# V2's first half ahead of the second chunk's first row, M's column reads on two queues, and the adding DMA on alternating tile rows

## The chip, the cores and the metric

The kernel runs on one core of a Trainium2 chip. Five engines take part: TensorE (PE in the profile; its weight loads are PEld), VectorE (DVE), ScalarE (ACT), GpSimd (POOL) and SyncE (SP), which issues most of the DMAs. Each engine works through its own instruction list in order; an instruction that waits holds up all that stand behind it on the same engine. DMAs are issued by an engine's queue and then run beside everything else. The metric is the device time of one execution in microseconds; the time given is the median of three runs.

## The reference, cut to what matters

The model is a compressed interaction network over x, a batch of 1024 with 64 features and 16 embedding columns.

```python
h = x0 = x                                     # (1024, 64, 16), float32
for i in range(3):                             # W0: 128 x 64*64, W1, W2: 128 x 64*64
    z = einsum('bfe,bge->bfge', x0, h)         # all products of a feature of x and one of h
    y = einsum('oc,bce->boe', W[i], z.reshape(b, -1, e)) + b[i]
    if i != 2: x_i, h = y[:, :64], y[:, 64:]   # one half is pooled, the other goes on
    else:      x_i = y                         # the last layer is pooled whole
    xs.append(x_i)
out = concat(xs, 1).sum(2) @ fc_w.T + fc_b     # pooled over e, then one number per batch row
```

The first layer's second half h1 is a quadratic form of x. Since the result is a weighted sum over all channels, the last layer can be folded ahead of time: V2 is W2 summed over its 128 output channels with their weights from fc_w, a 64 x 64 matrix, and M is V2 times the second half of W1, so that one more set of 64 quadratic forms of x, called q, stands for the second and third layers. What remains for each batch row is h1 and q (both x⊗x against fixed weights), their product summed over channels and columns, and some small terms.

## The kernel before, in words

**Tiles.** The batch is cut into 32 chunks of 32 rows, so a chunk has 512 columns (32 rows by 16 columns). For a chunk, `xa` holds 128 partitions by 4 by 512: the features, turned by i = 0 to 3. `xb` holds the features turned by 4 times j plus an offset, in four quarters of 128 by 512. A block z = xa * xb[j] (128 x 2048) has four tiles i; a *tile row* j is one block, and four rows hold all products that are needed. Fourteen blocks `z0` to `z13` are handed out in turn from a list (`take`, `used`). The weights `w_all` have 16 tiles (j, i) of 128 x 128: columns 0 to 63 give h1 (W0, made symmetric) and columns 64 to 127 give q (from M). All is float32; the profile shows each matmul as two passes.

**The head** deals with four chunks, in the order c0 to c3 = 2, 3, 0, 1, before M exists. For these only h1 is contracted: `product` (L240) makes a row on VectorE or GpSimd, and `half_contract` (L248; by columns for c0, L257) multiplies it with the first half of the weights. In between lies the making of q's weights:

- V2: eight matmuls in two halves n (L359), each of four matmuls of 32 columns of output partitions, with W2's half n as it was loaded (`w2s[n]`) as their moving operand. VectorE transposes each half's result (L364) into a block and copies the wanted rows into `v2t` (L371, with ScalarE at L372).
- M: eight matmuls of `v2t` with W1 (L387), evicted by ScalarE (L401) and written by DMA into a DRAM tensor `md` (L416 to L425).
- M is read back from `md` in the order of the tiles: `read_rows` (L469) and `read_columns` (L463) fill the two halves of `ms`, each DMA half of the partitions. VectorE adds the two (`q_weights`, L499) into the weights, a tile row at a time, and `head_q_tile` (L281) starts to use them for chunks 0 and 1, whose products are kept for it. `va` (features of M's diagonal) is read from `md` as well.

The code's order is each engine's order here: before the change `half_contract(c1, 0)`, the second chunk's first row, stands ahead of both halves of V2; row 0 and column 0 reads, and the row reads of rows 1 to 3, go out on SyncE and ScalarE, one half each; the six column reads of rows 1 to 3 and the read of `va` go out on SyncE behind `half_contract(c3, ...)`, ahead of the loads of chunk 4. Completion of these DMAs is counted on eight semaphores that are used in turn, so a DMA also waits for the one eight before it.

**The steady state.** From chunk 6 on, 26 chunks go in 13 pairs k = 3 to 15 (chunks a and b). For a pair, both quadratic forms of both chunks come from seven products of combined blocks with combined weights instead of eight: X, B21, B22, T3 are products from VectorE (`w_product`, L644, with sums of quarters at L650), and T2, T1, T4 are sums and differences of such blocks, made by GpSimd (`w_mix`, L661), in place where it can. T4 is used by `p4_run`, the run of matmuls into the PSUM bank `delta` with the first weights' half. Of T4's two tile rows GpSimd adds row 0 itself, and row 1 is added by a DMA that GpSimd issues (L659, `accum_op=add`, 1 MB). The operations of all pairs are put in a list by `at(when, ...)` and emitted in order of `when`; `when` is a position in units of one step, 31 steps to a pair. The table `mixed` holds a pair's seven mixes: T2 row 0, T2 row 1 in two parts, T1 rows 0 and 1, and last T4 row 0 at 18.5 and T4 row 1 at 18.6 (17.5 and 17.6 in the first pair). T4 is T2 with B21 added in place, so GpSimd's last work for a pair is its add of row 0, and then it issues the adding DMA for row 1. The first pair (k = 3) runs `first_window`; of the others those with even k run `a_leads` and those with odd k `o_leads`, which differ in which chunk's matmuls lead. In all, `p4_run`'s last four jobs (`LATE`), which are one tile row, go into the next pair (`first_fill`, `second_fill`).

All matmuls of the steady state go through `mm` (L530). `alpha`, `beta`, `gamma` and `delta` are PSUM banks, of which a pair of matmuls fills the two partition halves in turn.

Of the kernel before, what the change touches and what calls it, by code (L numbers as in the profile page):

```python
# [42 lines left out]
F = 64  # L43
# [7 lines left out]
NI = 4  # L51
NJ = 4
# [12 lines left out]
GROUPS = [(j, i) for j in range(2) for i in range(NI)]  # L65
# [5 lines left out]
def cin_kernel(ctx, tc, xra, xrb, wh, w0r, w1h, w2t, wx1, wx0, vec, lin, out):  # L71
    nc = tc.nc
# [6 lines left out]
    halves = [slice(0, F), slice(F, 128)]  # L79

    def const_tile(name, shape):
        return const.tile(shape, F32, tag=name, name=name)
# [4 lines left out]
    def take(uses=1):  # L87
        n = vacant.pop(0)
        left[n] = uses
        return n  # L90

    def used(n, times=1):
        left[n] -= times
        assert left[n] >= 0
        if left[n] == 0:
            vacant.append(n)
# [21 lines left out]
    for base in (0, 64, -64):  # L118
        nc.gpsimd.affine_select(
            out=shift, in_=shift, compare_op=ALU.not_equal, fill=1.0, base=base,  # L120
# [12 lines left out]
    va, vb, v0 = (const_tile(n, [128, F]) for n in ("va", "vb", "v0"))  # L133
# [8 lines left out]
    def load_xa(c, at=slice(0, NI)):  # L142
        if c not in xas or at.start == 0:
            xas[c] = xp.tile([128, NI, N], F32, tag="xa", name=f"xa_{c}")
        nc.sync.dma_start(  # L145
            out=xas[c][:, at, :],
            in_=bass.AP(
                tensor=xra.tensor, offset=c * XR * N + at.start * N,
                ap=[[N, 128], [1, (at.stop - at.start) * N]],
            ),  # L150
        )

    def quarter(c, j):
        xbs.setdefault(c, {})[j] = xp.tile([128, N], F32, tag="xb", name=f"xb_{c}_{j}", bufs=9)
        return xbs[c][j]

    def load_xb(c, *js):
        for j in js or range(NJ):
            nc.sync.dma_start(out=quarter(c, j), in_=xrb[c, :, j, :])
# [26 lines left out]
    c0, c1, c2, c3 = HEAD  # L186
# [49 lines left out]
    def product(c, j, first=0, last=NI, engine=nc.vector, uses=1):  # L236
        if first == 0:
            zs[c, j] = take(uses)
        at = slice(first, last)
        engine.tensor_tensor(  # L240
            blocks[zs[c, j]][:, at, :], xas[c][:, at, :],
            xbs[c][j].unsqueeze(1).to_broadcast([128, last - first, N]), ALU.mult,
        )

    def half_contract(c, *js, last=None):
        for j in js:
            for i in range(NI):
                nc.tensor.matmul(  # L248
                    accs[c][halves[i % 2]], w_all[:, j * NI + i, 0:64], blocks[zs[c, j]][:, i, :],
                    start=(j == 0 and i < 2), stop=(j == last and i > 1),  # L250
                )
            used(zs[c, j])
# [70 lines left out]
    for i in range(NI):  # L323
# [20 lines left out]
        out=linear, in_=bass.AP(tensor=lin.tensor, offset=lin.offset, ap=[[0, 128], [1, 384]])  # L344
# [2 lines left out]
    product(c1, NJ - 1, engine=nc.gpsimd)  # L347
    for j in (0, 1):
        product(c1, j)
    half_contract(c1, 0)  # L350


    v2b = take()
# [2 lines left out]
    for n in range(2):  # L356
        pv = ps.tile([128, 512], F32, tag=("set", "y")[n], name=f"pv2_{n}")
        for k in range(4):
            nc.tensor.matmul(  # L359
                pv[32 * k : 32 * k + 32], fv2, w2s[n][:, k * 512 : (k + 1) * 512],  # L360
                start=True, stop=True,
                tile_position=(0, 32 * k),
            )
        nc.vector.transpose(v2r[:, n, :], pv)  # L364
        used(w2b[n])


    v2q = v2r.rearrange("p n (s r) -> p (n s) r", r=32)[:, :, 0]
    for h in range(2):
        at = slice(32 * h, 32 * h + 32)  # L370
# [37 lines left out]
    row = EXT * F  # L408

    def m_ap(f1, f2, dims):  # L410
        return bass.AP(tensor=md.tensor, offset=md.offset + f1 * row + f2 * F, ap=dims)
# [3 lines left out]
    for half, queue in enumerate((nc.sync, nc.scalar)):  # L415
        queue.dma_start(  # L416
            out=m_ap(0, 32 * half, [[row, F], [1, 32 * F]]), in_=m_rows[halves[half]]
# [5 lines left out]
        out=m_ap(64, 68, [[row, 4], [4 * F, 7], [1, 4 * F]]),  # L423
        in_=m_rows[0:4, 4 * F :].rearrange("p (k c) -> p k c", c=4 * F),
# [29 lines left out]
    def skewed(f1, f2, dims):  # L454

        at = len(dims) - 2
        return m_ap(f1, f2, dims[:at] + [[row + F, F]] + dims[at:])
# [4 lines left out]
    def read_columns(j, queue, half):  # L462
        queue.dma_start(  # L463
            out=ms[halves[half], 1, j * NI : (j + 1) * NI],
            in_=skewed(0, 16 * half + 4 * (j + 1), [[row, NI], [1, F]]),
        )

    def read_rows(js, queue, half):
        queue.dma_start(  # L469
            out=ms[halves[half], 0].rearrange("p (j i) g -> p j (i g)", i=NI)[:, js],  # L470
            in_=skewed(
                16 * half + 4 * (js.start + 1), 0, [[4 * row, js.stop - js.start], [1, NI * F]]
            ),
        )

    for half, queue in enumerate(queues):
        read_rows(slice(0, 1), queue, half)
        read_columns(0, queue, half)
        read_rows(slice(1, NJ), queue, half)


    new_acc(c3)
# [2 lines left out]
    keep_h1(c2)  # L485
    half_contract(c3, 0, 3, 1, 2, last=2)

    for half in range(2):
        read_columns(1, nc.sync, half)
    for j in (2, 3):  # L490
        for half in range(2):
            read_columns(j, nc.sync, half)
    nc.sync.dma_start(out=va[halves[1]], in_=m_ap(0, 0, [[row + F, F], [1, F]]))
    load_xa(4)
    load_xb(4, 3, 0, 1, 2)

    def q_weights(j):
        at = slice(j * NI, (j + 1) * NI)
        nc.vector.tensor_tensor(w_all[:, at, 64:128], ms[:, 0, at], ms[:, 1, at], ALU.add)  # L499
# [20 lines left out]
    def at(when, fn, *args, **flags):  # L520
        ops.append((when, len(ops), fn, args, flags))
# [103 lines left out]
    FIRST_ROW, SECOND_ROW = GROUPS[:NI], GROUPS[NI:]  # L625

    def w_run(p, out, w, name, start=False, at_t=0, order=GROUPS):
        return [
            (w_job, p, out, w, j * NI + i + at_t, name, start and n == 0)
            for n, (j, i) in enumerate(order)  # L630
        ]
# [7 lines left out]
    wh_all, wq_all = w_all[:, :, 0:64], w_all[:, :, 64:128]  # L639
# [13 lines left out]
    def w_mix(p, j, out, in0, in1, first=0, last=NI):  # L653
        p.setdefault(out, {})
        if j not in p[out]:
            p[out][j] = p["X"][j] if j and p["k"] > 3 else take(9)
        o, x, y = p[out][j], p[in0][j], p[in1][j]
        if in1 == "B21" and j:
            nc.gpsimd.dma_start(out=blocks[o], in_=blocks[y], accum_op=ALU.add)  # L659
            return  # L660
        nc.gpsimd.tensor_tensor(  # L661
            *(blocks[b][:, first:last] for b in (o, x, y)),
            ALU.subtract if in1 == "T3" else ALU.add,
        )
        if last < NI:
            return
        for b in (x, y):
            if b != o:
                used(b)
# [26 lines left out]
    def make_pair(t, p, when, mixed):  # L696
        a, b = p["a"], p["b"]
        for when, c, j, name, uses in (
            (when[0], b, 2, "B22", 5), (when[1], b, 0, None, 0), (when[2], b, 0, "T3", 9),
            (when[3], a, 0, "X", 5), (when[4], b, 3, "B22", 5), (when[5], b, 1, None, 0),  # L700
            (when[6], b, 1, "T3", 9), (when[7], a, 1, "X", 13 if p["k"] > 3 else 5), (when[8], a, 2, "B21", 5),
            (when[9], a, 3, "B21", 5),
        ):
            if name is None:
                at(t + when, w_both, p, j)
                continue
            if name == "B21" and j == 2 and p["k"] == 3:
                at(t + when, w_product, p, c, j, name, uses, engine=nc.gpsimd)
                continue
            if name != "T3":  # L710
                ahead = 3.3 if p["k"] > 4 and name == "B22" and j == 2 else 2.7
                if p["k"] == 3 and name == "X" and j == 1:
                    ahead = 9.1
                at(t + when - ahead, second, c, j)
            at(t + when, w_product, p, c, j, name, uses)
        t2, t1, t4 = ("T2", "X", "T3"), ("T3", "B22", "T2"), ("T2", "T2", "B21")
        for when, j, names in zip(
            mixed, (0, 1, 1, 0, 1, 1, 0), (t2, (*t2, 0, 2), (*t2, 2), t1, t1, t4, t4)
        ):
            at(t + when, w_mix, p, j, *names)  # L720
        at(t + 29, lambda: used(p["B21"][1]))

    def p4_run(p):
        return w_run(p, delta, wh_all, "T2", at_t=2 * NI)

    def first_fill(p):
        return [(lambda: q_extra(p["a"], va, p["beta"]),)] + p4_run(p)[-LATE : -LATE // 2]

    def second_fill(p):
        return p4_run(p)[-LATE // 2 :]  # L730
# [149 lines left out]
    for n, p in enumerate(pairs):  # L880
        t = T0 + SPAN * n
# [54 lines left out]
    t, q = T0 + SPAN * NPAIR, pairs[-1]  # L936
# [184 lines left out]
```

## Time and profile before

| | us |
|---|---|
| median of three runs | 448.66 (447.75, 448.66, 449.8) |
| the profiled execution, its own time | 448.52 |
| its span | 446.7 |
| PE busy | 441.9 (99%) |
| DVE busy | 393.5 (88%) |
| POOL busy | 366.7 (82%) |
| ACT busy | 117.2 (26%) |
| POOL idle ahead of its mixes, released by PE | 28.8 (12 times) |
| xa load, 1024 KB, from issue to landing (median) | 8.9 |
| xb load, 256 KB | 8.5 |
| adding DMA, 1024 KB, 13 of them | 8.1 |
| DMA, mean | 224 GB/s |

The span is the time from the first to the last recorded instruction. In a timeline line the first number is the start in us from the span's start, the second the length, then the engine, the line, the operation, its output and inputs by name, its tile, its forms, and how many such instructions follow one another; in brackets stands the idle time of the engine just ahead and what ended it (`<-DVE z L240`: VectorE's write of a block at line 240). A matmul's end is modelled, its start is recorded, so the distance between starts tells the rate. The granted clock of TensorE is 0.9 and more in all slices of the page.

### The profile page before, as it was taken

The numbers are of one execution on the slowest core, as the hardware profiler recorded it, in microseconds if no ns is written. First come the engines' busy times: TensorE is split into PE (matmuls) and PEld (weight loads), VectorE is DVE, ScalarE is ACT, GpSimd is POOL, SyncE is SP. The second block draws the span as 40 slices with busy tenths as digits, with TensorE's granted clock in tenths as the row PEclk, the third lists the DMA queues.
The fourth block names the chain that finished last, engine by engine and source line by source line (L and its number), as shares of the span: only waits on it lengthen the run. The fifth ranks groups of instructions, "written<-read, shape, count | busy, mean of one in ns | idle before, by whom it ended". The sixth has DMA issues, their size and how long they took to land.

```text
span 446.7 us, 5944 instructions
## 1 busy us (share of the span) xinstructions
PE 441.9 (99%) x2234; PEld 151.8 (34%) x2234; DVE 393.5 (88%) x293; ACT 117.2 (26%) x215; POOL 366.7 (82%) x128
## 2 busy tenths in 40 slices
PE   9999999999999999999999999999999999999997
PEld 5333333333333333333333333333333333333345
DVE  4897699989989989999899979999899998999644
ACT  3163241332223123131312212231231313123211
POOL 5424788998997979799797979979797997979910
PEclk9999999999999999999999999999999999999999
DMA  8996998397949597694949769494976949692400
GB/s 299 416 343 151 331 412 342 93 346 133 357 117 295 167 221 273 137 360 102 303 158 234 268 128 357 105 312 149 232 264 133 372 92 286 223 240 86 98 1 0
DMA packets 35060, 99.85 MB, mean 224 GB/s; under 512 B 6389, under 2 KB 7189, under 8 KB 28441
## 3 DMA queue, kind: packets, MB, share of 16 engines
q1 hardware_dynamic: 32376, 84.90, 53.7%
q0 software_dynamic: 1872, 13.63, 17.4%
q10 hardware_dynamic: 784, 0.95, 0.8%
q8 instruction: 17, 0.28, 0.2%
q14 instruction: 11, 0.08, 0.0%
HBM read 84.20 MB, written 1.64 MB: 192 GB/s over the span
## 4 chain that ended last, share of the span: by engine, by line
PE 91%; DMA 6%; DVE 1%; SPq 0%; issue 0%; DVEq 0%
PE alpha L530 45%; PE delta L530 20%; PE beta L530 11%; PE acc L530 7%; PE q L530 3%; DMA xa<-in_xra 3%; PE acc L281 3%; DMA xb<-in_xrb 2%; PE acc L248 2%; DMA z<-in_w0r 1%; DVE z L240 1%; PE y L530 0%; SPq L145 0%; SPq L195 0%; PE hx L530 0%
## 5 line engine op out<-in xcount | busy, mean ns | idle before, releaser
L661 POOL TENSOR_TENSOR z<-z,z 128x2048 f32<-128x2048 f32 (+1 forms) x78 | 299.9, 3878 | 28.8 <-PE alpha L530 28.8
L530 PE MATMUL alpha<-z,ws 128*64 128x512 f32 x624 | 235.4, 593 | 0.0
L644 DVE TENSOR_TENSOR z<-xa,xp 128x2048 f32<-128x2048 f32 x103 | 231.5, 2279 | 1.2
L530 PEld LDWEIGHTS alpha<-z,ws 128*64 128x64 f32 x624 | 72.4, 137 | 91.0 <-issue 90.5
L530 PE MATMUL delta<-z,w_all 128*64 128x512 f32 x208 | 96.5, 592 | 0.0
L530 PE MATMUL alpha<-z,w_all 128*64 128x512 f32 x208 | 93.4, 593 | 0.0
L530 PE MATMUL beta<-z,w_all 128*64 128x512 f32 x208 | 92.7, 594 | 0.0
L530 PE MATMUL delta<-z,ws 128*64 128x512 f32 x208 | 91.4, 592 | 0.0
L558 ACT COPY xp<-xb 128x512 f32<-128x512 f32 x88 | 51.4, 587 | 127.4 <-DVE z L644 109.2
L240 DVE TENSOR_TENSOR z<-xa,xp 128x2048 f32<-128x2048 f32 (+1 forms) x29 | 45.5, 1619 | 4.3 <-ACT xp L558 3.2
L240 POOL TENSOR_TENSOR z<-xa,xb 128x2048 f32<-128x2048 f32 x6 | 28.2, 4760 | 17.5 <-DMA xb<-in_xrb 17.5
L530 PEld LDWEIGHTS delta<-z,w_all 128*64 128x64 f32 x208 | 28.4, 137 | 32.2 <-issue 32.2
L530 PEld LDWEIGHTS alpha<-z,w_all 128*64 128x64 f32 x208 | 28.1, 137 | 32.0 <-issue 29.5
L530 PEld LDWEIGHTS delta<-z,ws 128*64 128x64 f32 x208 | 28.5, 137 | 27.4 <-issue 25.7
L530 PEld LDWEIGHTS beta<-z,w_all 128*64 128x64 f32 x208 | 28.0, 137 | 27.4 <-issue 27.4
L530 PE MATMUL acc<-z,w_all 128*64 128x512 f32 x128 | 28.1, 592 | 0.0
L248 PE MATMUL acc<-z,w_all 128*64 128x512 f32 x96 | 21.6, 597 | 1.1 <-DVE z L240 1.1
L675 ACT ACTIVATE snap<-alpha,vs 64x512 f32<-64x512 f32 x13 | 8.9, 684 | 50.2 <-PE alpha L530 50.2
L682 DVE SCALAR_TENSOR_TENSOR snap<-alpha,vs,snap 64x512 f32<-64x512 f32 x13 | 9.7, 747 | 12.5 <-PE alpha L530 12.5
L672 ACT COPY snap<-alpha 64x512 f32<-64x512 f32 x13 | 7.6, 581 | 49.2 <-PE delta L530 34.9
L305 DVE TENSOR_REDUCE acc<-uu 128x64 f32<-128x1024 f32 (+2 forms) x19 | 19.6, 1036 | 0.2
L650 DVE TENSOR_TENSOR xp<-xp,xb 128x512 f32<-128x512 f32 x26 | 18.2, 699 | 0.8
(121 smaller groups left out, 357.6 us busy)
## 6 DMA issues: line engine op xcount, KB each, us to landing
xa<-in_xra SPq DMA_DIRECT2D x32, 1024.0 KB, 8.9
xb<-in_xrb SPq DMA_DIRECT2D x128, 256.0 KB, 8.5
z<-z POOLq DMA_DIRECT2D x13, 1024.0 KB, 8.1
e<-in_xra SPq DMA_DIRECT2D x28, 128.0 KB, 8.2
xx<-in_xra SPq DMA_DIRECT2D x28, 128.0 KB, 2.5
z<-in_w2t SPq DMA_DIRECT2D x2, 1024.0 KB, 8.4
z<-in_wx SPq DMA_DIRECT2D x2, 1024.0 KB, 9.9
xa<-in_xra SPq DMA_DIRECT2D x5, 256.0 KB, 4.3
```

The source lines that it names most:

```text
L240: engine.tensor_tensor(blocks[zs[c, j]][:, at, :], xas[c][:, at, :], xbs[c][j].unsqueeze(1).to_broadcast([128, last - first, N]), ALU.mult,)
L248: nc.tensor.matmul(accs[c][halves[i % 2]], w_all[:, j * NI + i, 0:64], blocks[zs[c, j]][:, i, :], start=(j == 0 and i < 2), stop=(j == las ...
L281: nc.tensor.matmul(accs[c][halves[1 - c % 2]], w_all[:, t, 64:128], blocks[zs[c, j]][:, i, :], start=(t == 0), stop=False, skip_group_chec ...
L305: nc.vector.tensor_reduce(acc[rows, of, k, half], uu[rows, of if at is None else at, E * half.start : E * half.stop].rearrange("p k (b e) ...
L530: nc.tensor.matmul(out, w, rhs, start=start, stop=stop, skip_group_check=True)
L558: nc.scalar.copy(bank, xbs[c][j])
L644: engine.tensor_tensor(blocks[b], xas[c], xbs[c][j].unsqueeze(1).to_broadcast([128, NI, N]), ALU.mult)
L650: nc.vector.tensor_tensor(bank, bank, xbs[p["b"]][j], ALU.add)
L661: nc.gpsimd.tensor_tensor(*(blocks[b][:, first:last] for b in (o, x, y)), ALU.subtract if in1 == "T3" else ALU.add,)
L672: nc.scalar.copy(snaps[0][p["O"]], alpha(p))
L675: nc.scalar.activation(snaps[1][p["O"]], alpha(p), AF.Identity, bias=bh1[p["A"]])
L682: nc.vector.scalar_tensor_tensor(hb_, alpha(p), bh1[p["A"]], hb_, ALU.add, ALU.add)
```

## The change: what it does

1. `half_contract(c1, 0)` is taken from ahead of V2 and stands now between V2's two halves: the order on TensorE becomes V2's first half, the second chunk's row 0, V2's second half.
2. The column reads of rows 1 to 3 stand in the loop over the two queues, behind each queue's row reads: SyncE reads half 0, ScalarE half 1. All are ahead of `half_contract(c3, ...)` in the code. The read of `va` goes from ahead of the loads of chunk 4 to behind them.
3. Which row of T4 is added by DMA alternates: row 0 in odd pairs, row 1 in even ones as before (`p["k"] % 2 ^ 1`). Since row 0's place (18.5) is ahead of row 1's (18.6), in odd pairs the DMA is issued ahead of GpSimd's own add. `p4_run` takes the second row first in odd pairs, and the block that the DMA read is given back accordingly.

```diff
     for j in (0, 1):
         product(c1, j)
-    half_contract(c1, 0)
...
         nc.vector.transpose(v2r[:, n, :], pv)
         used(w2b[n])
+        if n == 0:
+            half_contract(c1, 0)
...
         read_rows(slice(0, 1), queue, half)
         read_columns(0, queue, half)
         read_rows(slice(1, NJ), queue, half)
+        for j in range(1, NJ):
+            read_columns(j, queue, half)
...
     half_contract(c3, 0, 3, 1, 2, last=2)
 
-    for half in range(2):
-        read_columns(1, nc.sync, half)
-    for j in (2, 3):
-        for half in range(2):
-            read_columns(j, nc.sync, half)
-    nc.sync.dma_start(out=va[halves[1]], in_=m_ap(0, 0, [[row + F, F], [1, F]]))
     load_xa(4)
     load_xb(4, 3, 0, 1, 2)
+    nc.sync.dma_start(out=va[halves[1]], in_=m_ap(0, 0, [[row + F, F], [1, F]]))
...
         o, x, y = p[out][j], p[in0][j], p[in1][j]
-        if in1 == "B21" and j:
+        if in1 == "B21" and j == p["k"] % 2 ^ 1:
             nc.gpsimd.dma_start(out=blocks[o], in_=blocks[y], accum_op=ALU.add)
             return
...
-        at(t + 29, lambda: used(p["B21"][1]))
+        at(t + 29, lambda: used(p["B21"][p["k"] % 2 ^ 1]))
 
     def p4_run(p):
-        return w_run(p, delta, wh_all, "T2", at_t=2 * NI)
+        order = SECOND_ROW + FIRST_ROW if p["k"] % 2 else GROUPS
+        return w_run(p, delta, wh_all, "T2", at_t=2 * NI, order=order)
```

## The prediction

> **What bounds the kernel now.** I read four views in this order: the page, the chain of work that ended last, the timelines of single engines at the three places of the edit, and the waits.
>
> ```profile
> span 446.7 us, 5944 instructions
> PE 441.9 (99%) x2234; PEld 151.8 (34%) x2234; DVE 393.5 (88%) x293; ACT 117.2 (26%) x215; POOL 366.7 (82%) x128
> PE 91%; DMA 6%; DVE 1%; SPq 0%; issue 0%; DVEq 0%
> ```
>
> TensorE is busy 99% of the span and is 91% of the chain. A busy matmul engine may still be slow, so I looked at its start times. A pair of 64-column matmuls, each shown as two passes, starts a pass every 0.43 us (263.15, 263.57, 264.00 below), and from 36 us to the end I find no step longer than that except where the tile shape changes (some 0.10 us each). So from 36 us on the time is the matmul count; whatever is made earlier there shortens nothing. What can be won lies in the first 36 us. TensorE's and VectorE's timelines there:
>
> ```profile
> 17.56 1.94 PE L248 MATMUL acc<-z,w_all 128*64 128x512 f32 x8 [0.83 <-DVE z L240]
> 19.43 1.92 PE L359 MATMUL pv<-z,fv 128*32 128x512 f32 x16
> 21.28 3.65 PE L248 MATMUL acc<-z,w_all 128*64 128x512 f32 x16
> ...
> 35.94 1.51 PE L248 MATMUL acc<-z,w_all 128*64 128x512 f32 x6 [0.26 <-DVE z L240]
> ```
>
> ```profile
> 20.56 1.57 DVE L364 STREAM_TRANSPOSE z<-pv 128x512 f32<-128x512 f32 x2 [0.95 <-PE pv L359]
> 22.17 0.40 DVE L371 COPY res<-z 64x32 f32<-64x32 f32 x2
> 22.59 2.29 DVE L240 TENSOR_TENSOR z<-xa,xp 128x2048 f32<-128x2048 f32 x1
> 24.80 6.69 DVE L240 TENSOR_TENSOR z<-xa,xb 128x2048 f32<-128x2048 f32 x3
> 31.41 6.68 DVE L240 TENSOR_TENSOR z<-xa,xp 128x2048 f32<-128x2048 f32 x3
> ```
>
> The reader is to see a handover. TensorE idles 0.83 us before 17.56 for the second chunk's first product. VectorE then idles 0.95 us, to 20.56, for V2's matmuls, and from there works without a gap to 40.3. TensorE's wait at 35.94 is for a product of that row. So VectorE from 20.56 sets when TensorE gets its last late operand, and what makes the transposes earlier makes everything behind 35.94 earlier.
>
> Third, the steady state, an odd pair (k = 9): GpSimd, then two rows of TensorE.
>
> ```profile
> 246.74 13.58 POOL L661 TENSOR_TENSOR z<-z,z 128x2048 f32<-128x2048 f32 x3
> 260.25 0.85 POOL L659 DMA_DIRECT2D z<-z  x1
> 260.86 4.84 POOL L661 TENSOR_TENSOR z<-z,z 128x2048 f32<-128x2048 f32 x1
> 268.11 4.71 POOL L661 TENSOR_TENSOR z<-z,z 128x1024 f32<-128x1024 f32 x2 [2.41 <-PE alpha L530]
> ```
>
> ```profile
> 262.72 0.59 PE L530 MATMUL delta<-z,w_all 128*64 128x512 f32 x1
> 263.15 0.59 PE L530 MATMUL delta<-z,w_all 128*64 128x512 f32 x1
> 263.57 0.59 PE L530 MATMUL delta<-z,w_all 128*64 128x512 f32 x1
> 264.00 0.59 PE L530 MATMUL delta<-z,w_all 128*64 128x512 f32 x1
> ...
> 270.44 0.59 PE L530 MATMUL delta<-z,w_all 128*64 128x512 f32 x1
> ```
>
> ```profile
> DMA to landing us min/median/max: 6.9/8.1/8.7
> ```
>
> GpSimd waits 2.4 us per pair for TensorE (28.8 us over 12 times in the waits), so it has that much room in a period of 26.06 us. The adding DMA is issued at 260.25, lands 8.1 to 8.7 us later (268.4 to 269.0), and TensorE first uses its row at 270.44: 1.4 to 2.1 us of room. In even pairs the row is first used 13.6 us behind the issue (247.82 against 234.19), which leaves 4.9 us and more.
>
> **The change, part by part.** The sum is made against the profiled execution, 448.52 us (span 446.7 and 1.82 around it), 0.14 under the median 448.66 of the three runs.
>
> *V2's first half.* Nothing is added; four matmuls (8 of the 16 passes at 19.43, two steps of 0.43 = 0.86 us) move ahead of the eight passes at 17.56. Their operand, the first half of W2, was issued at 6.04 and landed 8.4 us later (14.5); TensorE is free at 16.56. They start there, with 0.10 us for the change of shape, and end at 16.56 + 0.10 + 0.86 + 0.10 = 17.62, the last term for changing back. The second chunk's row, ready at 17.56, thus starts 0.06 us later. V2's second half follows 1.87 us behind (19.43 - 17.56), at 19.49 instead of 20.31, so 0.82 us earlier; its operand came by 16.95, when SyncE stopped waiting for it. On VectorE the product that ends at 19.6 comes first, then the first transpose (0.72, its input long ready), then the second, released at 21.39 - 0.82 = 20.57: the whole row behind it moves by 0.82. I looked for what is late next: the loads of the third chunk landed at 22.66 and 23.33, its product now starts at 23.98; the fourth chunk's at 27.86 and 28.53, ScalarE's copy of it ends at 29.3, its product starts at 32.8; GpSimd's product of the fourth chunk ends at 35.93 and TensorE reads it at 36.8 (1.7 us behind 35.1). All hold. Gain 0.82 us; ends: 0 (a load is late after all) and 0.99 (the idle time 16.56 to 17.56).
>
> The row comes first for a rule too. Entering V2's shape costs 0.52 instead of 0.43 us (18.90 to 19.43). The Trainium skill, "TensorEngine Tiling (Array Packing)", section Key Properties, says that changing the tiling mode drains the engine, which speaks against splitting V2: two more changes, 0.20 us by these rows. The sum above holds both, one of them inside idle time; without the rule or with it the sum is the same.
>
> *M's column reads.* Three of SyncE's six reads (0.57 to 0.62 us of issue each) go to ScalarE's queue, all ahead of hb and snap of the third chunk (39.58). ScalarE issues the like in 0.89 to 1.08 us, so that pair waits some 1.8 to 3.2 us, to at most 42.8. Behind it stands the same pair of the fourth chunk (43.07, held by TensorE) and behind that VectorE's sum at 46.07, after which VectorE idles 3.2 us until 51.76: that covers it. SyncE's next load goes from 43.98 to about 42.2, the landing of the row read whose completion semaphore it reuses (one of eight, in turn). va's read moves behind five loads (2 MB, some 5 us): from 46.7 to about 51 to 52; GpSimd needs it at 56.04. The weights of M's first tile row (40.81 + 0.43 = 41.24) are needed by TensorE at 42.86 - 0.82 = 42.04; the second (43.95) at 42.04 + 3.43 = 45.5. TensorE does not wait here before, so the 1.8 us are worth 0; bounds: no gain is possible, a loss of up to 0.4 if the first row's reads land 1.2 us later.
>
> The DMA share is 1.01 to 1.05 from 50 to 75 us, whoever issued. The Trainium skill, "DMA: Bandwidth & Descriptors", section Issuing engines are not separate DMA queues, agrees in general: two issuing engines save issue time alone. By it this part would be worth the three issues, 1.8 us on SyncE, and none of it on the path.
>
> *The adding DMA.* In odd pairs (7 of 13) row 0 of T4 is added by DMA and row 1 by GpSimd, and TensorE takes row 1 first. GpSimd's three operations behind 246.74 become two and the issue: at 255.77, where today's add of row 0 starts without a wait, 4.5 us earlier than now. Landing 264.5 instead of 268.7, used at 270.44: room 5.9 us instead of 1.8. GpSimd's add of row 1 then waits for TensorE's last pass over the old row 1 (alpha, 255.97 + 0.59 = 256.56) and takes 4.57: 261.2, needed at 262.72, 1.5 us to spare. The next operation starts at 261.2 instead of 260.86, which the wait of 2.41 absorbs. In the first pair the room is 106.30 - 100.9 - 4.57 = 0.8 us. In the last pair two steps of other work are missing: TensorE's last pass over the old row ends at 412.94, 412.95 + 4.57 = 417.5, needed at 417.92: 0.4 us. An add beside an issue took 4.84 instead of 4.57, which still fits. Worth 0, ends -0.3 (lost in the last pair) and a gain only where an execution today has a late DMA. SyncE's loads from 262 us (chunk 22) come out from behind the adding DMA; the DMA share was 0.00 from 258 to 260, so nothing new collides.
>
> Sum: 448.52 - 0.82 = 447.7 us; on the median of the runs 448.66 - 0.82 = 447.8. A change under 0.5% (2.2 us) can hardly be told from none here.
>
> **The rivals.**
> *No gain (the head is bound by loads).* For it: the chain names DMA ahead of 29.91. Against it: VectorE has no gap from 22.59 to 40.3, so no load stopped it. It would give 448.6.
> *Slower: GpSimd's add of row 1 becomes late in odd pairs.* It is now pinned behind TensorE's read and has 1.5 us. If the new wait is as long as today's longest on GpSimd (2.5 us) instead of the 0.25 us from 256.38 to 256.6, row 1 is ready at 256.38 + 2.5 + 4.57 = 263.45, 0.73 late, seven times: +5.1 - 0.8, 453. It decides from 1.5 us on. Against it: the read's end is in the trace.
> *Faster: today's odd-pair DMA is late in unprofiled executions.* Room is 1.4 to 2.1 us and the runs spread over 2.05 us (447.75 to 449.8). If the median carries six landings that are 0.2 us late, 1.2 us more go: 446.6; at 0.4 us, 445.4. Against it: no such wait in the profiled execution, which sits on the median.
>
> **How the numbers follow.** Forecast 0.72 (447.8, own range 447.0 to 448.4), no gain 0.10, late add 0.06, late DMA today 0.12. Two thirds of that last case lie beyond 0.5% (under 446.4). Hence faster 0.08, same 0.86, slower 0.06. The range leaves out the slower rival and the far end of the faster one: 446.5 to 449.2, the upper end being the median plus 0.3 for the last pair and some spread.
>
> **What would show it.** PE: pv at about 16.6 and 19.5, no idle 0.83, the row of 35.94 at about 35.1. DVE: second transpose at about 20.6. ACT: five reads from md, hb at 41 to 43. POOL in odd pairs: issue, then an add, with a wait of some 0.3 us between; the rest of the wait per pair 2.0 us. PE after 36 us still 0.43 us a step. Wrong it is if steps over 0.43 us appear at delta's first passes in odd pairs or at the head's second tile row, or if the row of 35.94 does not move.

## The result, and the profile after

The changed kernel takes 447.4 us (median of 22 executions, 447.03 to 448.27) where the kernel before, on the same chip, takes 448.41 (22 executions, 447.75 to 449.8). The ratio is 0.9979, 95% interval 0.9972 to 0.9985: by this ratio 0.94 us less, between 0.67 and 1.26. The forecast was 447.8 and 0.82 us less. The profiled execution took 447.38, with a span of 445.6.

The page after, first its span, its engines' busy times and its chain by engine:

```profile
span 445.6 us, 5946 instructions
PE 441.4 (99%) x2234; PEld 151.3 (34%) x2234; DVE 394.2 (88%) x293; ACT 117.3 (26%) x215; POOL 368.0 (83%) x128
PE 92%; DMA 6%; DVE 1%; SPq 0%; issue 0%; DVEq 0%
```

TensorE's timeline in the head of the kernel after (L358 is V2's matmuls, L281 the first use of M's weights):

```profile
15.88 1.07 PE L358 MATMUL pv<-z,fv 128*32 128x512 f32 x8
16.88 1.94 PE L248 MATMUL acc<-z,w_all 128*64 128x512 f32 x8
18.75 1.06 PE L358 MATMUL pv<-z,fv 128*32 128x512 f32 x8
...
34.91 7.09 PE L248 MATMUL acc<-z,w_all 128*64 128x512 f32 x32 [0.26 <-DVE z L240]
41.83 8.75 PE L281 MATMUL acc<-z,w_all 128*64 128x512 f32 x40
```

And VectorE's:

```profile
18.54 0.71 DVE L363 STREAM_TRANSPOSE z<-pv 128x512 f32<-128x512 f32 x1
19.88 0.72 DVE L363 STREAM_TRANSPOSE z<-pv 128x512 f32<-128x512 f32 x1 [0.63 <-PE pv L358]
...
21.07 2.29 DVE L240 TENSOR_TENSOR z<-xa,xp 128x2048 f32<-128x2048 f32 x1
23.76 6.70 DVE L240 TENSOR_TENSOR z<-xa,xb 128x2048 f32<-128x2048 f32 x3 [0.41 <-DMA xb<-in_xrb]
30.38 2.28 DVE L240 TENSOR_TENSOR z<-xa,xp 128x2048 f32<-128x2048 f32 x1
```

The idle time of 0.83 us ahead of the second chunk's row is gone, and the row of 35.94 stands at 34.91. But the whole head of this execution is earlier: V2's first half starts at 15.88 where I had put it at 16.6. And there is a new wait: 0.41 us for a load of the third chunk, at 23.76. So the 1.03 us cannot be read as the gain of the move; the table in the next section parts the two.

GpSimd in the odd pair k = 9, after (L657 issues the adding DMA, L659 adds):

```profile
241.04 13.74 POOL L659 TENSOR_TENSOR z<-z,z 128x1024 f32<-128x1024 f32 x4 [2.46 <-PE alpha L528]
254.72 0.83 POOL L657 DMA_DIRECT2D z<-z  x1
255.70 9.18 POOL L659 TENSOR_TENSOR z<-z,z 128x2048 f32<-128x2048 f32 x2 [0.15 <-PE alpha L528]
267.08 18.28 POOL L659 TENSOR_TENSOR z<-z,z 128x1024 f32<-128x1024 f32 x5 [2.21 <-PE alpha L528]
```

The issue stands ahead of the add, with a wait of 0.15 us between, and 2.21 us of the pair's wait are left (forecast some 0.3 and 2.0). The add of row 1 ends 4.57 us behind 255.70, at 260.27; TensorE takes row 1 at 261.69 and row 0 at 269.41, in steps of 0.43. The DMA's row lands 7.6 us behind the issue, at 262.3. ScalarE issues six reads from `md` (I had counted five) and its pair of copies of the third chunk starts at 41.51. From the first matmul at L281 to the last of TensorE, the profiles before and after both take 400.89 us: in these two executions TensorE neither gains nor loses between these points. Behind its last matmul the span goes on for 2.72 us before and 2.61 after. That 0.11 us was not forecast. ScalarE's two drains at the end of the program, before and after (shortest, median and longest in ns; the shortest is the last):

```profile
L1117 ACTq DRAIN  x2: 142/227/312, 443.4 to 446.4; - x2
```

```profile
L1116 ACTq DRAIN  x2: 14/160/307, 442.4 to 445.1; - x2
```

The last one takes 0.142 us before and 0.014 after. The experiments below show which part of the change this belongs to.

### The profile page after: what moved, and what is told of

The parts are those of the page before. It is cut to its first block, busy times and chain, and to the rows that moved or that the text cites. A ratio compares the mean times of both kernels' runs of the same rounds, so it can differ in the third digit from the quotient of the medians.

```text
span 445.6 us, 5946 instructions
## 1 busy us (share of the span) xinstructions
PE 441.4 (99%) x2234; PEld 151.3 (34%) x2234; DVE 394.2 (88%) x293; ACT 117.3 (26%) x215; POOL 368.0 (83%) x128
## 4 chain that ended last, share of the span: by engine, by line
PE 92%; DMA 6%; DVE 1%; SPq 0%; issue 0%; DVEq 0%
PE alpha L528 45%; PE delta L528 20%; PE beta L528 11%; PE acc L528 7%; DMA xa<-in_xra 3%; PE q L528 3%; PE acc L281 3%; DMA xb<-in_xrb 2%; PE acc L248 2%; DMA z<-in_w0r 1%; DVE z L240 1%; PE y L528 0%; SPq L145 0%; SPq L195 0%; PE hx L528 0%
## 5 line engine op out<-in xcount | busy, mean ns | idle before, releaser
L659 POOL TENSOR_TENSOR z<-z,z 128x2048 f32<-128x2048 f32 (+1 forms) x78 | 298.6, 3856 | 28.6 <-PE alpha L528 27.4
L240 POOL TENSOR_TENSOR z<-xa,xb 128x2048 f32<-128x2048 f32 x6 | 27.3, 4560 | 17.9 <-DMA xb<-in_xrb 17.8
L305 DVE TENSOR_REDUCE acc<-uu 128x64 f32<-128x1024 f32 (+2 forms) x19 | 19.6, 1036 | 0.2
```

The lines of the kernel that those rows point to most:

```text
L240: engine.tensor_tensor(blocks[zs[c, j]][:, at, :], xas[c][:, at, :], xbs[c][j].unsqueeze(1).to_broadcast([128, last - first, N]), ALU.mult,)
L305: nc.vector.tensor_reduce(acc[rows, of, k, half], uu[rows, of if at is None else at, E * half.start : E * half.stop].rearrange("p k (b e) ...
L659: nc.gpsimd.tensor_tensor(*(blocks[b][:, first:last] for b in (o, x, y)), ALU.subtract if in1 == "T3" else ALU.add,)
```

## The experiments

All of them run beside the kernel before on the same chip. Where several experiments are compared, their medians are set against all 107 executions of the kernel before that these runs hold (448.38).

### Each part alone

*V2's move alone:*

```diff
         product(c1, j)
-    half_contract(c1, 0)
...
         used(w2b[n])
+        if n == 0:
+            half_contract(c1, 0)
```

> The kernel before with V2's first half alone moved ahead of the second chunk's row 0. Theory (handover in the head): all of the change's gain is here, -0.8 us (-0.6 to -1.1) against the kernel before; VectorE's second transpose ends about 1.5 us behind the first instead of directly behind it, and its row of products starts about 0.8 us earlier against the start of the second chunk's products, unless it then waits for a load of chunk c2. Rival (adding DMA late in executions without a profile): this part gives -0.4 us or less, and the rest lies in the adding DMA. Rival (bound by loads): 0 to -0.3, with VectorE waiting for the load.

Measured: 447.95 us (12 executions, 447.47 to 450.07), ratio 0.9993 (0.9981 to 1.0005).

*The column reads alone* (the second part of the change):

```diff
         read_rows(slice(1, NJ), queue, half)
+        for j in range(1, NJ):
+            read_columns(j, queue, half)
...
-    for half in range(2):
-        read_columns(1, nc.sync, half)
-    for j in (2, 3):
-        for half in range(2):
-            read_columns(j, nc.sync, half)
-    nc.sync.dma_start(out=va[halves[1]], in_=m_ap(0, 0, [[row + F, F], [1, F]]))
     load_xa(4)
     load_xb(4, 3, 0, 1, 2)
+    nc.sync.dma_start(out=va[halves[1]], in_=m_ap(0, 0, [[row + F, F], [1, F]]))
```

> The kernel before with the column reads alone on two queues and va's read behind the loads. All theories: 0 (-0.15 to +0.15); the second row's weights are wanted on time in both. If the reads matter after all, -0.3 or +0.4 us.

Measured: 447.87 us (12 executions, 447.31 to 448.67), ratio 0.9992 (0.9981 to 1.0004).

*The adding DMA alone:*

```diff
-        if in1 == "B21" and j:
+        if in1 == "B21" and j == p["k"] % 2 ^ 1:
...
-        at(t + 29, lambda: used(p["B21"][1]))
+        at(t + 29, lambda: used(p["B21"][p["k"] % 2 ^ 1]))
...
-        return w_run(p, delta, wh_all, "T2", at_t=2 * NI)
+        order = SECOND_ROW + FIRST_ROW if p["k"] % 2 else GROUPS
+        return w_run(p, delta, wh_all, "T2", at_t=2 * NI, order=order)
```

> The kernel before with the adding DMA alone taking row 0 in odd pairs. Theory (handover in the head): 0 (-0.2 to +0.3), since neither the DMA nor GpSimd's add is late. Rival (adding DMA late in executions without a profile): -0.5 to -1.0 us. Rival (GpSimd's add late): +2 to +5 us, with steps over 0.43 us at delta's passes in odd pairs.

Measured: 448.33 us (12 executions, 447.6 to 448.79), ratio 0.9997 (0.9987 to 1.0007).

*V2 whole ahead of the row:*

```diff
         product(c1, j)
-    half_contract(c1, 0)
...
         used(w2b[n])
+        if n == 1:
+            half_contract(c1, 0)
```

> The kernel before with both halves of V2 ahead of the second chunk's row 0. Theory (handover, and the loads as the next bound): V2's second half starts when its operand has landed (17 to 18 us), VectorE no longer waits for V2, and the second transpose ends some 0.5 us earlier than with half of it moved; but c2's loads (landed 23.3 to 23.7) then stop VectorE. So -0.8 to -1.1 us against before, within 0.3 of the half move. Without the bound by loads it would be 0.4 to 0.6 us beyond the half move.

Measured: 448.0 us (12 executions, 447.13 to 454.74; four of them, at 449.11, 450.33, 454.73 and 454.74, lie more than 1 us above the median), ratio 0.9997 (0.9982 to 1.0011). VectorE's wait for V2 is gone, it then waits 0.28 us for the third chunk's load, and TensorE comes to M's first weights at 42.12, 7.12 us behind the start of the last row ahead of them instead of 6.91: 0.2 us late. In the measure of the table below this profile takes 24.82, 0.71 less than without a move, where half of V2 gave 0.85: here the second half was worth nothing more.

The times alone do not part the theories: the intervals are as wide as the effects. The traces do. VectorE in the profile of V2's move alone:

```profile
19.86 0.71 DVE L363 STREAM_TRANSPOSE z<-pv 128x512 f32<-128x512 f32 x1
20.90 0.72 DVE L363 STREAM_TRANSPOSE z<-pv 128x512 f32<-128x512 f32 x1 [0.32 <-PE pv L358]
```

And TensorE in the columns alone, where the idle time ahead of the second chunk's row is shorter than in the profile before:

```profile
16.72 1.94 PE L248 MATMUL acc<-z,w_all 128*64 128x512 f32 x8 [0.62 <-DVE z L240]
```

The table takes each profile's head from a point that the change does not touch, the start of the second chunk's second product on VectorE (P), to the first matmul at L281:

| profile | P | L281 | between | VectorE's wait for c2's load |
|---|---|---|---|---|
| before | 17.33 | 42.85 | 25.52 | 0 |
| columns alone | 16.49 | 42.03 | 25.54 | 0 |
| adding DMA alone | 17.07 | 42.60 | 25.53 | 0 |
| before, late head | 19.48 | 45.02 | 25.54 | 0 |
| before, delayed issue | 16.77 | 42.31 | 25.54 | 0 |
| V2 alone | 17.67 | 42.35 | 24.68 | 0 |
| without the columns | 17.37 | 42.11 | 24.74 | 0 |
| whole change again | 17.13 | 42.12 | 24.99 | 0 |
| V2 alone, late head | 18.85 | 43.85 | 25.00 | 0 |
| whole change, late head | 18.21 | 43.21 | 25.00 | 0 |
| whole change | 16.34 | 41.83 | 25.48 | 0.41 |
| whole change, delayed add | 16.79 | 42.22 | 25.43 | 0.50 |

Without the move it is 25.53 to a hundredth or two. With it, three cases: 0.85 and 0.79 us less, 0.53 to 0.54 less (three times), 0.05 and 0.10 less. The mean of the seven is 0.48. The full 0.85 needs the idle time of 0.83 us that the profile before had ahead of the second chunk's row. Four of the five profiles without the move have 0.61 or 0.62 there; then V2's first half, which takes 1.00 us with its two changes of shape, does not fit and pushes the row back by some 0.3. The profiles with the move agree. Without it the row starts 0.23 us behind P in all five. From the start of V2's first half to P + 0.23 it is 1.01 and 0.93 us in the two profiles that gained 0.85 and 0.79, and 0.68 to 0.69 in the three that gained 0.53 to 0.54. And where the head is early (P at 16.3 to 16.8), VectorE gets to the third chunk before its load, which landed at 23.3 to 24.1 in the profiles with the normal head.

P itself lies between 16.34 and 17.67 with one and the same head code. That is the start of the kernel: of the 1.14 us between the profiled executions before and after, 0.99 are P, 0.04 this stretch and 0.11 the end. The last section comes back to it.

The end belongs to the column reads. From the last matmul to the end of the span it is 2.72 us in all eight profiles without them, and 2.59 to 2.61 in five of the six with them (in the sixth, the row on GpSimd below, an output lands some 0.67 us later; its last drain is as short). ScalarE's last drain takes 0.14 us in the eight and 0.014 in the six. Why the reads on ScalarE's queue make it short is not shown.

### A late head

```diff
-    for n in (128,) * 6 + (64,):
+    for n in (128,) * 14 + (64,):
```

> The kernel before with eight more of the first, empty 128-column matmuls (L114) on TensorE, which makes the head's matrix work late against the loads, whose times stay. No theory of the change is at stake in its own time: some 449 to 450.5 us. From the end of the second chunk's second product on VectorE to the first matmul with M's weights (L281) it should take 23.25 us, as in the profiles of the kernel before, of the columns alone and of the adding DMA alone.

> The same late head, with V2's first half moved and nothing else changed. Theory (the move gives 0.85 us where the loads of chunk c2 leave room, and less where the head is early and VectorE then waits for them): the full 0.85 us against the late head without the move (0.65 to 1.0); the stretch from the second chunk's second product to L281 takes 22.4 us and VectorE does not wait for a load. Rival (the measured gain of the whole change lies in the column reads or the adding DMA): 0.4 us or less.

> The same late head with the whole change. Theory: the same as with V2's move alone (within 0.2 us), 0.85 us under the late head of the kernel before. Rival (column reads or adding DMA give the rest): 0.3 to 0.6 us below V2's move alone.

Measured: 451.73 us (449.93 to 456.66) for the kernel before, 451.25 (449.73 to 455.74) for V2 alone and 449.67 (448.41 to 456.16) for the whole change. The stretch of the table was 25.54, 25.00 and 25.00, with no wait for a load. So the move gave 0.54, not the 0.85 that I expected, for the reason of the 0.61 us hole. With 9, 8 and 12 executions that spread over 6 to 8 us, the first two medians decide nothing. The 1.58 us between the last two are nearer to the rival than to the theory, and the profile of V2's move alone shows one cause. TensorE at the first pair's use of the adding DMA's row, in that profile:

```profile
114.63 0.59 PE L531 MATMUL beta<-e,va 128*64 128x512 f32 x1
...
117.23 0.64 PE L531 MATMUL delta<-z,w_all 128*64 128x512 f32 x1 [2.00 <-DMA z<-z]
...
118.87 1.06 PE L531 MATMUL alpha<-z,ws 128*64 128x512 f32 x1
...
119.72 1.06 PE L531 MATMUL alpha<-z,ws 128*64 128x512 f32 x1
```

and by stretches (window in us; its length; TensorE's busy time and matmuls; granted clock; DMA share; GB/s):

```profile
114.50:117.20 2.70, 0.73 (x4) 1.00 0.84 325
117.20:118.50 1.30, 1.26 (x6) 0.91 1.10 326
118.50:121.40 2.90, 2.90 (x8) 0.50 1.04 384
121.40:130.00 8.60, 8.60 (x42) 0.98 0.45 163
```

The adding DMA landed 2.0 us late, and behind the wait TensorE's granted clock was 0.50 for some 3 us, with steps of 0.85 instead of 0.43. The stretch from L281 to the last matmul is 404.81 instead of 400.89, so this one landing cost 3.9 us, the wait included. The Trainium skill, "TensorE: Matmul & The Clock Gate", Part 1, says that TensorE runs at half rate after an idle window of about 3.4 us and needs a busy one to come back; the half rate and its length agree, but here a wait of 2.0 us was enough.

Why it was late is seen in the issues, GpSimd's and SyncE's, in the first pair. Before:

```profile
104.18 0.94 POOL L659 DMA_DIRECT2D z<-z  x1
106.11 0.33 SPq L145 DMA_DIRECT2D xa<-in_xra  x1
```

V2 alone with the late head:

```profile
106.17 0.94 POOL L660 DMA_DIRECT2D z<-z  x1
107.10 0.33 SPq L145 DMA_DIRECT2D xa<-in_xra  x1
```

SyncE's next load followed 1.9 us behind and the adding DMA landed after 8.49 us; 1.4 behind, after 8.99 (columns alone); 1.3 behind, after 9.56 (before, late head, 0.18 us late); 0.9 behind, after 11.02. So without the alternation, the closer the loads follow, the longer the adding DMA takes. With it, the loads ahead count too, by these rows. The whole change again, first pair:

```profile
97.71 0.95 POOL L657 DMA_DIRECT2D z<-z  x1
```

This one took 12.03 us although SyncE's next load followed only 7.7 us behind; but SyncE's last load ahead of it was issued no more than 2.0 us before (95.69 to 96.83 for two), and the DMA share was 1.04 from 95 to 100 us. Without the columns the last loads went out from 94.68 to 95.82, the DMA at 100.28, and it took 6.99. Still, the row of the 12.03 us landed at 109.74 and is wanted at 113.33. In the seven profiles with the alternation the first pair's DMA took 7.0 to 12.2 us and landed 3.6 to 6.6 us ahead of its use. Without the alternation, and without a delay or a late head, it landed 0.4 us (columns alone) to 1.4 us ahead. So what the alternation gives the first pair is not a faster DMA but an issue some 4 to 6 us earlier.

### Delays on GpSimd

Two operations whose result nothing uses, in odd pairs: in the kernel before ahead of the DMA's issue, in the changed kernel behind it and ahead of the add:

```diff
+        if in1 == "B21" and j and p["k"] % 2:
+            for _ in range(2):
+                nc.gpsimd.tensor_tensor(linear, linear, linear, ALU.subtract)
```

> The kernel before with two idle-value operations on GpSimd (a 128x384 tile minus itself, some 2.05 us together) directly ahead of the issue of the adding DMA in odd pairs. Theory (the DMA's time from issue to landing is fixed at some 8.5 us): rooms of 1.40, 1.72, 1.79, 1.78, 1.81 and 1.47 us in the first six odd pairs are overrun by 0.65, 0.33, 0.26, 0.27, 0.24 and 0.58, +2.3 us in all. Rival (the DMA collides with SyncE's next loads, whose issue comes 1.9 us behind it now and would then come at the same time; at 0.9 us the first pair's took 11.0 us): each of the six landings is some 5 us late, +10 to +40 us, and TensorE runs at half rate for some steps behind each long wait.

Measured: 480.15 us, ratio 1.0707 (1.0689 to 1.0725). The rival holds. GpSimd's and SyncE's issues in pair k = 9, and TensorE's waits behind 100 us (in total, times, longest):

```profile
277.02 1.74 POOL L660 TENSOR_TENSOR linear<-linear 128x384 f32<-128x384 f32 x2
278.71 0.86 POOL L662 DMA_DIRECT2D z<-z  x1
```

```profile
278.88 0.33 SPq L145 DMA_DIRECT2D xa<-in_xra  x1
```

```profile
PE delta L530 <- DMA z<-z: 22.8, 6, 4.7
```

A delay of 1.74 us brought the issue onto the loads. The six landings took 12.1 to 12.6 us instead of 8.4 to 8.7, TensorE waited 3.8 us for each, and it lost another 1.6 us a time at half rate, in steps of 0.85 us ((436.06 - 403.88 - 22.8)/6, from L281 to the end of the span).

> The changed kernel with the same two operations on GpSimd at the same place, which in odd pairs is now behind the DMA's issue and ahead of GpSimd's add of row 1. Theory (the prediction's room of 1.5 us for that add, by the profile after 1.42, in the first pair 0.7, in the last 0.3): row 1 is late by 0.63 five times, 1.35 in the first pair and 1.75 in the last, +6.3 us against the changed kernel; the DMA's row is on time. Rival (the add has more room than read): +0 to +2.

Measured: 450.54 us, ratio 1.0044 (1.0028 to 1.0061), 3.1 us above the changed kernel; 2.8 of it lie between L281 and the last matmul (403.68 instead of 400.89). GpSimd in pair k = 9, and TensorE's wait:

```profile
255.67 0.81 POOL L660 DMA_DIRECT2D z<-z  x1
256.28 1.97 POOL L658 TENSOR_TENSOR linear<-linear 128x384 f32<-128x384 f32 x2
258.20 9.19 POOL L662 TENSOR_TENSOR z<-z,z 128x2048 f32<-128x2048 f32 x2
```

```profile
PE delta L528 <- POOL z L662: 1.2, 1, 1.2
```

The add starts 2.53 us behind the issue instead of 0.98, that is 1.55 later, against a room of 1.42 in the profile after. Row 1 cost TensorE 0.2 to 0.3 in each of five pairs, 1.4 in the last and nothing in the first. I had expected twice the loss, because I counted the delay as 2.05. The room itself is as read, and no landing hurt.

### A version meant to be faster

The last row of the third chunk on GpSimd, which stands idle there:

```diff
-    xb2 = ps.tile([128, N], F32, tag="set", name=f"xp_{c2}_{NJ - 1}")
-    nc.scalar.copy(xb2, xbs[c2][NJ - 1])
-    xbs[c2][NJ - 1] = xb2
...
-    for j in range(NJ):
+    for j in range(NJ - 1):
         product(c2, j, uses=1 + NI)
+    product(c2, NJ - 1, engine=nc.gpsimd, uses=1 + NI)
...
-    half_contract(c2, *range(NJ), last=3)
+    half_contract(c2, 0, 1, 3, 2, last=2)
```

> The changed kernel with the last row of chunk c2 made by GpSimd, which is idle from 17 to 31 us, instead of VectorE; its copy to PSUM on ScalarE, which held M's eviction back until the load came (25.7 us), goes. Theory (VectorE's row of products, and behind it M's way through DRAM, bound the head): TensorE's two waits at 32.7 and 34.9 us (0.43 and 0.43 us of lengthened steps) go, M's weights come 1 us or more earlier, and L281 starts at 40.7 to 41.3 instead of 41.83: -0.5 to -1.1 us against the changed kernel, 446.3 to 446.9. Rival (M's way through DRAM is bound by the loads ahead of it, and the weights are not earlier): TensorE waits for them instead, -0.1 to -0.5.

Measured: 454.71 us, ratio 1.0139 (1.0123 to 1.0154): neither theory saw this. M did come back earlier (the row reads from `md` were issued at 36.14 instead of 37.31), but VectorE, which makes the weights of it, was slowed and started that at 45.78 instead of 40.85. The three products of the third chunk in this kernel:

```profile
23.90 15.36 DVE L240 TENSOR_TENSOR z<-xa,xb 128x2048 f32<-128x2048 f32 x3
```

GpSimd's first product beside them:

```profile
25.98 4.60 POOL L240 TENSOR_TENSOR z<-xa,xb 128x2048 f32<-128x2048 f32 x1 [8.60 <-PE pcx L397]
```

and, in the changed kernel, GpSimd's one product in this stretch:

```profile
30.96 4.57 POOL L240 TENSOR_TENSOR z<-xa,xb 128x2048 f32<-128x2048 f32 x1 [14.15 <-DMA xb<-in_xrb]
```

VectorE's products with `xb`, both operands in SBUF, took 6.70 us for three in the changed kernel (23.76 above) and 15.36 here: 2.30 for the first, and 6.62 and 6.60 for the two with GpSimd at work beside them from 25.98 on. In the changed kernel VectorE's products beside GpSimd's are those with `xp`, whose second operand ScalarE has copied to PSUM, and they take 2.28 each (30.38 above). The Trainium skill, "GPSIMD Engine Reference", section 8, says that GpSimd shares its SBUF interfaces with VectorE and contends with its instructions of two SBUF inputs; the rows agree. So the copy that I took away carried the row.

### The change without the column reads, and the whole again

V2's move and the adding DMA's alternation, `read_columns` as before the change, that is the first and the third diff of this section together; and beside it the whole change once more:

> V2's move and the adding DMA's alternation, with M's column reads as before the change. Theory (the column reads are worth nothing; the move gives 0.5 to 0.85 us less what the loads of c2 take back; the alternation takes away the late landings in the first pair that lengthen single executions): the same median as the whole change within 0.25 us, 447.2 to 447.7, and no execution over 448.6 us, while the move alone had three of twelve over it (448.63, 449.11, 450.07). Rival (the column reads have a share of the gain): 0.3 to 0.6 us above the whole change.

> The whole change, run beside the kernel without the column reads. 447.4 us (447.2 to 447.7), -0.7 to -1.2 against the kernel before, and no execution over 448.6 us. If the first result was chance, -0.3 to -0.6.

Measured: 447.79 us (11 executions, 447.43 to 448.36), ratio 0.9986 (0.9976 to 0.9996), and 447.62 (447.07 to 448.02), ratio 0.9980 (0.9972 to 0.9989). The medians lie 0.17 apart (95% by resampling -0.10 to 0.68), inside the theory, and of that the end of the program, 2.72 against 2.60 us in these two profiles, is 0.12. But the profile without the column reads shows a wait that the theory excluded: from L281 to the last matmul it takes 401.47 instead of 400.89. VectorE, ScalarE and TensorE there:

```profile
53.15 4.48 DVE L240 TENSOR_TENSOR z<-xa,xp 128x2048 f32<-128x2048 f32 x2 [4.81 <-ACT xp L559]
```

```profile
81.50 0.47 ACT L551 ACTIVATE va<-shift 64x32 f32<-64x32 f32 x2 [1.72 <-DVE shift L546]
```

```profile
81.34 0.59 PE L531 MATMUL acc<-e,vs 64*64 64x512 f32 x1
82.02 0.65 PE L531 MATMUL acc<-e,va 128*64 128x512 f32 x2
```

TensorE takes `va` at 82.02, 0.68 behind the last matmul, where it was 0.52 (82.08 to 82.60) in the profile before: `va` was ready only at 81.97. It then loses 0.4 us more at 85.0, by the order of the rows because VectorE has yet to read a PSUM bank (its reduction at L305 starts at 84.89 instead of 83.52). VectorE is late because its products of chunk 4 began at 53.15 instead of 51.76, with the load. ScalarE's first copy of that load, before and without the column reads:

```profile
51.14 0.59 ACT L558 COPY xp<-xb 128x512 f32<-128x512 f32 x1 [6.79 <-DMA xb<-in_xrb]
```

```profile
52.53 0.59 ACT L559 COPY xp<-xb 128x512 f32<-128x512 f32 x1 [8.93 <-DMA xb<-in_xrb]
```

SyncE issued the loads of chunk 4 at the same time in both (from 43.98 and 44.02), so this load was some 1.4 us slower in this execution. The move does not explain that: with V2 alone the same copy starts at 50.67. The room at `va` in the eight profiles with the old reads and a normal order of rows is 2.01, 1.98, 1.61, 1.48, 1.26, 1.01, 0.84 and 0.05 us; in the five with the new reads 1.73, 2.26, 2.31, 2.49 and 2.71. The move makes TensorE earlier while this load stays where SyncE sends it (43.75 to 44.1 us in the profiles with the normal head), so it takes some of the room: it would have come to `va` at 81.86, 0.74 us earlier than before. But `va` was ready 1.38 us later than before (81.97 instead of 80.59), and that is the slow load; only the two together exceed the room of 2.01. The column reads send the load at 42.1 to 42.7; that this would have covered the loss is an argument, not a run. In the other seven of the eight the room was not used up.

## Why the prediction was right, point by point

*V2's first half: the mechanism right, the size the best case.* The sum of 0.82 us, with its steps (0.10, 0.86, 0.10, and the row 0.06 later), is what V2's move shows where the hole is no smaller than in the profile before: 0.85 and 0.79. The step that failed is to take the idle time of one execution, 0.83, as the kernel's; in most it is 0.61, and then the term is 0.54. "All hold" failed as well: in two of seven profiles the third chunk's load came 0.41 and 0.50 us late and took back nearly all. The rival of the loads, which I gave 0.10, was weighed by VectorE having no gap in one execution. The room between that load and its product, 1.47 us there (23.33 to 24.80), is 0.57 with the adding DMA alone (23.97 to 24.54) and 0.22 with the columns alone (23.75 to 23.97). The term's mean is 0.48.

*The column reads: the bound "no gain is possible" was wrong.* They gave 0.12 us at the end of the program, where I had not looked. And my cover was VectorE's idle time up to 51.76. But that idle time is the wait for the very load that SyncE sends behind the reads: it is no cover, it is the chain. Its end has 0.8 to 2.0 us of room at 82 us in seven profiles and 0.05 in one, which lost 0.58; I did not follow it that far.

*The adding DMA: 0 in every undisturbed execution, as predicted.* The alternation alone is at 448.33 against 448.38. The places were right: DMA room, GpSimd's room of 1.5 (measured 1.42, and 0.3 in the last pair, where the delay cost most). The rival of late DMAs exists, but in another form than I priced it: not six landings of 0.2 to 0.4 us, but a first pair that can collide with the loads and then costs up to 3.9. Of 107 executions of the kernel before, 8 lie more than 1 us above their median, 2 of 12 with V2's move alone and 4 of 12 with V2 whole ahead; of the 12 with the column reads alone none, and of the 56 with the alternation and the normal head (it alone, without the columns, and the whole change twice) none. The rooms of 0.4 to 1.4 us against 3.6 and more in the first pair would fit this. But that the first pair is the cause is shown only for the late head, and there 2 of 12 executions of the whole change lie that far out as well (451.38 and 456.16).

*The sum.* 0.82 + 0 + 0 met 0.94 because two errors offset each other, which is luck. Against the kernel before, medians (95% by resampling): V2 alone -0.43 (-0.69 to 0), V2 and the adding DMA -0.59 (-0.90 to -0.24), the whole -0.92 (33 executions, -1.11 to -0.72), columns alone -0.51 (-0.88 to +0.22), adding DMA alone -0.06 (-0.33 to +0.34). So some 0.45 us is V2's move, as in the table, and 0.5 (0.2 to 0.9) comes with the two parts that I put at nothing. Of that the traces show 0.12, the column reads at the end of the program. Some 0.3 us stays open: the profiles of the whole change with the normal head differ from those of the kernel before in P, the stretch of the table and the end, and in nothing else that TensorE feels. Rarer losses of the kernel before that the change takes away, at `va` and in the first pair, are candidates, and so is chance in P; no run decides.

## What to carry to other kernels

A hole that the profile shows is that of one execution; before a move is sized by it, look at what sets its two ends, and at whether a load or the start of the kernel moves one of them. Idle time covers a delay only if what ends it does not itself come later by that delay: name the releaser before counting the idle time as room. A transfer's time from issue to landing holds for the traffic that it met, so a delay of its issue can cost several times its own length (1.74 us of delay cost some 5.3 a time here), and a wait of 2.0 us on TensorE cost almost as much again at half rate. And follow a change to the end of the program: here 0.12 us lay behind the last matmul.

## What had not been expected

The start of the kernel is not the same in each execution. TensorE's steps of four matmuls at L218 are 0.85 to 0.91 us up to a moment that differs, and 0.43 from there: up to some 6.4 us in the profile before, 6.65 with V2 alone, 5.7 with the adding DMA alone, 4.5 after. The granted clock reads 1.00 throughout there, so only the steps show it. The later that moment, the later is P in these four (17.33, 17.67, 17.07 and 16.34): a spread of 1.3 us, more than the whole change. The Trainium skill, "TensorE: Matmul & The Clock Gate", Part 1, says that the window is free-running and the warm-up differs from run to run; the profiles agree. One execution of the whole change with the late head, 456.16 us, lies far above the others and no profile shows why; that stays open.
